# Order of VectorE's first work: two score tiles ahead of the second pair's residues, both value projections after the sixth tile

## Chip, cores and metric

The kernel runs on 1 core of a Trainium2 chip. The metric is the device time of one execution, in microseconds (us).

## What is computed

One transformer layer on x of 32 sequences x 256 tokens x 128 features, in float32: attention of 16 heads of 8 features with a causal mask and a distance penalty, then a gated feed-forward block of width 512, each followed by a residual sum and a layer norm. Cut to what matters here:

```python
Q = split_heads(x @ Wq.T + bq); K = split_heads(x @ Wk.T + bk); V = split_heads(x @ Wv.T + bv)
scores = jnp.einsum('bhid,bhjd->bhij', Q, K) / jnp.sqrt(jnp.float32(hd))
scores = jnp.where(causal_mask, -jnp.inf, scores) + decay
attn = jax.nn.softmax(scores, axis=-1)
out = jnp.einsum('bhij,bhjd->bhid', attn, V)
```

## The kernel before, in words

The 32 sequences are worked in 16 pairs; a pair is 512 tokens. Five engines take part, each in the order in which the program names its work: TensorE (PE), VectorE (DVE), ScalarE (ACT), GpSimd (POOL) and SyncE (SP, which issues most of the DMAs; ScalarE's queue issues the others). The wrapper `InOrder` (L50) keeps PE, DVE, ACT and SP in program order, and every instruction made through it carries the line L58 in the profile, so that one goes by the names of tiles.

**Queries and keys.** `project(n)` (L314) transposes a pair's x (`pxT`), copies it to SBUF on VectorE (`xT`), and multiplies it by the weights into `pq` and `pk`. `halves` (L295) splits each product into a leading part (`qhi`, `khi`, on ScalarE) and a residue (`qlo`, `klo`, on VectorE, which reads the product and the leading part). `stack` (L305) then spreads the four tiles by eight DMAs of 256 KB over interleaved rows of the big operands `qs` and `ks`: two for each of `qhi` and `qlo` on SP's queue, two for each of `khi` and `klo` on ScalarE's. Every score matmul contracts over all of these rows. Beforehand `fill` (L185) writes the constant rows.

**Row maxima.** A softmax needs each row's maximum first. `row_maxima(n, i)` (L373), with i from 0 to 11, computes one score tile (four matmuls of 62x128 by 62x256, or eight of 62x128 by 62x128 where i mod 3 is 2; then four small masking matmuls with `tri_q`) and reduces it on VectorE into `m`. `maxima_to_rows` (L407) transposes `m` (`pm`), splits it into `mhi` (ScalarE) and `mlo` (VectorE) and writes both into rows of `qs` by DMAs on SP. `weigh` (L430) then computes the scores again with the maxima in them, takes the exponential on ScalarE (`e`) and masks on GpSimd; `outputs` (L470) multiplies by the values.

**Values.** `project_values(n)` (L339) makes eight matmuls of 128x128 into `pv`; VectorE adds the bias in four instructions into `vaug`.

**Buffers.** Score tiles lie in three PSUM buffers (`ps_s`, L283) of 128x1024; `pxT`, `pq`, `pk`, `pv`, `pm` and the like share two buffers of 128x512 (`ps_w`, L284). So a fourth score tile waits for the first one's reduction, and a third `work` tile waits until the first has been read. The leading parts and residues of pair 1 lie in the pool `setup`, which is closed at L704; its memory is used again by `ep`, `op`, `yp` and `once`, the last of which takes the feed-forward weights.

**The start** (L684 to L720) is written out by hand. For VectorE, the order is: the operands of pair 0, `fill(qs[1])` (L694), the residues of pair 1 (within `run(ahead)`, L695), the values of pair 0 (L698), six tiles of maxima of pair 0 (L710), the values of pair 1 (L712), `maxima_to_rows(0, (0,))` (L713), `load_layers` (L714, the weights, on SP), six more tiles (L715), `maxima_to_rows(0, (1,))`, and two tiles of pair 1. After that `step(0)` begins, in which the pair's twelve `weigh` tiles alternate with pair 1's maxima, pair 2's projection (`project(2)`) and a count of weights that float32r can't hold (`differ`); then a branch, and steps 1 to 15.

Of the kernel before, what the change touches and what calls it, by code (L numbers as in the profile page):

```python
# [8 lines left out]
F32 = mybir.dt.float32  # L9
# [4 lines left out]
ALU = mybir.AluOpType  # L14
# [47 lines left out]
def tile_attn_ffn(  # L62
# [24 lines left out]
    pe, vec, act, sp = (InOrder(tc, e) for e in (nc.tensor, nc.vector, nc.scalar, nc.sync))  # L87
# [97 lines left out]
    def fill(dst, nm, eng, groups=slice(0, W)):  # L185
        t, base = fills[nm]
        to = dst[:, groups, :]
        t = t.unsqueeze(1).to_broadcast([P, groups.stop - groups.start, TOK])
        if eng is act:
            act.activation(to, t, AF.Identity, bias=base)  # L190
        else:
            eng.tensor_scalar(to, t, base, None, ALU.add)
# [93 lines left out]
    def work(nm):  # L286
        return ps_w.tile([P, 512], F32, name=nm, tag="work")

    def two(nm):
        return ps_s.tile([P, 2, 512], F32, name=nm, tag="s")  # L290
# [4 lines left out]
    def halves(n, ps, bias, nm):  # L295
        pool = setup if n == 1 else hlp
        hi = pool.tile([P, TOK], F32R, name=f"{nm}hi_{n}", tag=f"{nm}hi")
        act.activation(hi, ps, AF.Identity, bias=bias)
        lo = pool.tile([P, TOK], F32R, name=f"{nm}lo_{n}", tag=f"{nm}lo")
        vec.scalar_tensor_tensor(  # L300
            lo, ps, bias, hi.bitcast(F32), ALU.add, ALU.subtract
        )
        return hi, lo

    def stack(n, nm, eng=sp):  # L305
        for r, part in {
            "q": ((0, 0), (1, 0), (2, 1), (3, 1)), "k": ((0, 0), (2, 0), (1, 1), (3, 1))
        }[nm]:
            eng.dma_start(
                out=pairs[n][nm][PAIRING + r :: W, :, :].bitcast(F32),  # L310
                in_=pairs[n][nm + "s"][part].bitcast(F32),
            )

    def project(n):  # L314
        xn = xs[n]
        if n + 1 < NPAIR:
            xs[n + 1] = load_x(n + 1)
        pt = work(f"pxT_{n}")
        for t in range(NT):
            pe.transpose(pt[:, t * P : (t + 1) * P], xn[:, t, :], ident)  # L320
        xT = xtp.tile([P, TOK], F32, name=f"xT_{n}", tag="xT", bufs=2)
        vec.tensor_copy(xT, pt)

        for t in range(NT):
            nc.gpsimd.tensor_tensor(xn[:, t, :], xn[:, t, :], bo_sb, ALU.add)
        yield
        pq = work(f"pq_{n}")
        pe.matmul(pq, lhsT=wq_sb, rhs=xT, start=True, stop=True)
        q = halves(n, pq, bq_sb, "q")
        yield  # L330
        pk = work(f"pk_{n}")
        pe.matmul(pk, lhsT=wk_sb, rhs=xT, start=True, stop=True)
        k = halves(n, pk, bk_sb, "k")
        m = mp.tile([P, 2, 2, H], F32, name=f"m_{n}", tag="m")
        pairs[n] = dict(
            q=qs[n % 2], k=ks[n % 2], qs=q, ks=k, m=m, xT=xT, xb=xs.pop(n)
        )

    def project_values(n):  # L339
        xT, v = pairs[n]["xT"], vaug[n % 2]  # L340
        pairs[n]["v"] = v
        pv = work(f"pv_{n}")
        for t in range(NT):
            pe.matmul(
                pv[:, t * D : (t + 1) * D], lhsT=xT[:, t * P : (t + 1) * P], rhs=wv_sb,
                start=True, stop=True,
            )
        to = v[:, :, 0 : H // 2 * VSLOT].rearrange("p t (r c k) -> p t r c k", r=2, c=C)
        src = pv.rearrange("p (t r e c d) -> p t r e c d", t=NT, r=2, e=2, c=C)
        bias = bv_sb.rearrange("p (r e c d) -> p r e c d", r=2, e=2, c=C)  # L350
        for r in range(2):
            for e in range(2):
                vec.tensor_tensor(
                    to[:, :, r, :, 2 * e * VHEAD : 2 * e * VHEAD + HD], src[:, :, r, e],
                    bias[:, r, e].unsqueeze(1).to_broadcast([P, NT, C, HD]), ALU.add,
                )
# [3 lines left out]
    def mask(blocks):  # L360


        for p, f in ((0, 0), (1, 1), (0, 1), (1, 0)):
            s, first, count = blocks(p)
            rows = slice(64 * p, 64 * p + 64)
            pe.matmul(
                s[64 * f : 64 * f + 64, :, first + 64 * f : first + 64 * f + 64],
                lhsT=ident_b[rows, rows],
                rhs=tri_q[rows, rows].unsqueeze(1).to_broadcast([64, count, 64]),
                start=False, stop=True, tile_position=(64 * p, 64 * f),  # L370
            )

    def row_maxima(n, i):  # L373

        q, k, m = (pairs[n][w] for w in "qkm")
        mv = m.rearrange("i b c (e p g) -> i e p g b c", e=2, p=2)[:, i // 6]
        a, part = divmod(i, 3)
        if part < 2:
            g = 2 * a + part
            s = two(f"s1_{n}_{g}").rearrange("i p (b j) -> i p b j", b=2)  # L380
            for b in range(2):
                for p in range(2):
                    rows = slice(64 * p, 64 * p + ROWS1)
                    pe.matmul(
                        s[:, p, b, :], lhsT=q[rows, g, b * T + P : (b + 1) * T],
                        rhs=k[rows, g, b * T : (b + 1) * T], start=(b == 0), stop=False,
                    )
            mask(lambda p: (s[:, p], P, 2))
            vec.tensor_reduce(mv[:, :, g % C, :, 1], s, AX.X, ALU.max, negate=True)
            return  # L390
        s = two(f"s1_{n}_{a}d").rearrange("i p (h b j) -> i p h b j", h=2, b=2)
        for h in range(2):
            for b in range(2):
                for p in range(2):
                    rows = slice(64 * p, 64 * p + ROWS1)
                    i0 = b * T
                    pe.matmul(
                        s[:, p, h, b, :], lhsT=q[rows, 2 * a + h, i0 : i0 + P],
                        rhs=k[rows, 2 * a + h, i0 : i0 + P],
                        start=(h == 0 and b == 0), stop=False,  # L400
                    )
        mask(lambda p: (s[:, p].rearrange("i h b j -> i (h b) j"), 0, 4))
        vec.tensor_reduce(
            mv[:, :, 2 * a % C : 2 * a % C + 2, :, 0], s, AX.X, ALU.max, negate=True
        )

    def maxima_to_rows(n, halves=(0, 1)):  # L407

        q, m = pairs[n]["q"], pairs[n]["m"]
        pm = work(f"pm_{n}_{halves[0]}")  # L410
        e0, rows = halves[0], W * len(halves)
        for t in range(NT):
            pe.transpose(
                pm[0:rows, t * P : (t + 1) * P],
                m[:, t // 2, t % 2, W * e0 : W * e0 + rows], ident,
            )
        hi = mp.tile([H, TOK], F32R, name=f"mhi_{n}_{e0}", tag="mhi", bufs=1)
        act.copy(hi[0:rows, :], pm[0:rows, :])
        lo = mp.tile([H, TOK], F32R, name=f"mlo_{n}_{e0}", tag="mlo", bufs=1)
        vec.tensor_tensor(  # L420
            lo[0:rows, :], pm[0:rows, :], hi[0:rows, :].bitcast(F32), ALU.subtract
        )
        for i, e in enumerate(halves):
            for r, part in enumerate((hi, lo)):
                sp.dma_start(
                    out=q[ROWS1 + r :: 64, C * e : C * e + C, :].bitcast(F32),
                    in_=part[W * i : W * i + W, :].bitcast(F32),
                )
# [250 lines left out]
    def run(gen):  # L679
        for _ in gen:  # L680
            pass
# [11 lines left out]
    next(ahead)  # L693
    fill(qs[1], "q", vec)  # L694
    run(ahead)  # L695
    stack(1, "q", sp)
    stack(1, "k", act)
    project_values(0)  # L698
    for a in range(G):
        act.dma_start(  # L700
            out=wo_sb[C * HD * a : C * HD * (a + 1), :],
# [5 lines left out]
    yp = enter(tc.tile_pool(name="yp", bufs=2))  # L707
    lctx = ctx.enter_context(ExitStack())
    once = lctx.enter_context(tc.tile_pool(name="once", bufs=1))
    for i in range(6):  # L710
        row_maxima(0, i)
    project_values(1)  # L712
    maxima_to_rows(0, (0,))  # L713
    loaded = load_layers(once)  # L714
# [166 lines left out]
```

## Time and profile before

| | us |
|---|---|
| median of 3 runs (823.79 to 824.07) | 823.96 |
| the profiled execution's own time | 824.06 |
| its span, first to last instruction | 822.2 |
| PE busy in the span | 784.6 (95%) |
| DVE busy | 636.0 (77%) |
| ACT busy | 527.5 (64%) |
| PE busy from 11.0 to 20.7 us of the span | 5.55 of 9.70 |
| DVE busy in the same stretch | 5.07 of 9.70 |

A row of the timeline has the start in us from the span's start, the duration in us, the engine, the line, the operation, the tile written and those read with their shapes, and xN for N instructions merged; in brackets stands how long the engine had been idle before and what ended that. A row of the DMA view has a queue (q1 is fed by SP, q10 by ScalarE), packets, MB and the share of the 16 DMA engines' time. A row of the stage view has a stretch, its length, then for each engine the busy time in it, then the granted clock of TensorE (1.00 is full), the DMA share and GB/s.

### The profile page before, as it was taken

The numbers are of one execution on the slowest core, as the hardware profiler recorded it, in microseconds if no ns is written. First come the engines' busy times: TensorE is split into PE (matmuls) and PEld (weight loads), VectorE is DVE, ScalarE is ACT, GpSimd is POOL, SyncE is SP. The second block draws the span as 40 slices with busy tenths as digits, with TensorE's granted clock in tenths as the row PEclk, the third lists the DMA queues.
The fourth block names the chain that finished last, engine by engine and source line by source line (L and its number), as shares of the span: only waits on it lengthen the run. The fifth ranks groups of instructions, "written<-read, shape, count | busy, mean of one in ns | idle before, by whom it ended". The sixth has DMA issues, their size and how long they took to land.

```text
span 822.2 us, 17431 instructions
## 1 busy us (share of the span) xinstructions
PE 784.6 (95%) x7046; PEld 555.8 (68%) x7046; DVE 636.0 (77%) x1247; ACT 527.5 (64%) x719; POOL 260.8 (32%) x341
## 2 busy tenths in 40 slices
PE   4896999999999999999999999999999999999994
PEld 2664676776767677676767767676767767666673
DVE  6786778877887887778788877888878787873674
ACT  5065556766666766766576676667666666758572
POOL 5033413333142333414232342424243231424211
PEclk9879999999999999999999999999999999999998
DMA  6824140403204140410404040130404022000001
GB/s 147 213 62 106 29 92 14 106 15 74 60 14 106 28 107 14 92 42 21 110 17 106 27 101 20 43 90 15 107 26 104 4 62 59 14 4 14 1 8 37
DMA packets 39898, 47.49 MB, mean 58 GB/s; under 512 B 3968, under 2 KB 21632, under 8 KB 39808
## 3 DMA queue, kind: packets, MB, share of 16 engines
q1 hardware_dynamic: 37152, 42.82, 22.0%
q10 hardware_dynamic: 2656, 3.48, 1.9%
q8 instruction: 57, 0.93, 0.5%
q14 instruction: 33, 0.27, 0.1%
HBM read 7.48 MB, written 4.19 MB: 14 GB/s over the span
## 4 chain that ended last, share of the span: by engine, by line
PE 83%; DVE 4%; ACT 3%; issue 1%; DMA 0%; POOL 0%; ACTq 0%; POOLq 0%; DVEq 0%
PE peven L58 14%; PE podd L58 14%; PE s L58 12%; PE pa L58 11%; PE pw L58 10%; PE s_2d L58 2%; PE s_3d L58 2%; PE po L58 2%; PE s_0d L58 2%; PE s_1d L58 2%; PE pt L58 2%; PE pv L58 2%; PE pk L58 2%; PE pq L58 2%; PE px1T L58 1%; PE py L58 1%
## 5 line engine op out<-in xcount | busy, mean ns | idle before, releaser
L58 DVE TENSOR_REDUCE m<-s 128x4 f32<-128x1024 f32 x128 | 155.5, 1218 | 14.6 <-PE s L58 13.3
L58 ACT ACTIVATE e<-s 128x1024 f32<-128x1024 f32 x128 | 130.7, 1022 | 44.2 <-PE s L58 34.2
L463 POOL TENSOR_SCALAR_AFFINE_SELECT e<-e 128x512 f32<-128x512 f32 x128 | 82.6, 646 | 218.5 <-ACT e L58 189.3
L58 PE MATMUL podd<-h,h_near 128*128 128x512 f32 x512 | 131.3, 403 | 1.0 <-DVE m L58 0.5
L58 PE MATMUL peven<-hodd,h_near 128*128 128x512 f32 x512 | 122.7, 396 | 0.0
L58 PEld LDWEIGHTS peven<-hodd,h_near 128*128 128x128 f32 x512 | 95.7, 187 | 23.4 <-DVE hodd L58 0.3
L58 PEld LDWEIGHTS podd<-h,h_near 128*128 128x128 f32 x512 | 91.8, 188 | 23.1 <-DVE h L58 3.2
L58 ACT ACTIVATE hodd<-podd,sh 128x512 fp32r<-128x512 f32 x64 | 44.0, 688 | 62.7 <-PE podd L58 62.6
L58 PE MATMUL pw<-x1T,w_near 128*128 128x512 f32 x256 | 75.6, 418 | 1.1 <-DVE h0w L58 1.1
L274 POOL TENSOR_TENSOR rsa<-rsa,half 128x4 f32<-128x4 f32 x16 | 16.3, 1018 | 176.7 <-DVE rsa L58 176.7
L58 DVE SCALAR_TENSOR_TENSOR h0w<-pw,s,sg 128x512 f32<-128x512 f32 x64 | 47.9, 748 | 30.4 <-ACT sg L58 30.4
L58 PEld LDWEIGHTS s<-qs,ks 64*128 64x128 f32 x512 | 38.9, 188 | 47.7 <-issue 34.1
L58 PE MATMUL pa<-e,vaug 128*32 128x256 f32 x1024 | 70.6, 389 | 0.0
L58 PE MATMUL s<-qs,ks 64*128 64x256 f32 x512 | 65.3, 335 | 0.6 <-ACT e L58 0.5
L58 DVE TENSOR_TENSOR heven<-evenw,heven 128x512 fp32r<-128x512 f32 x64 | 44.2, 692 | 26.6 <-ACT evenw L58 26.1
L58 ACT ACT_TABLE_LOAD x47 | 60.3, 1283 | 3.4 <-issue 2.6
L58 ACT ACTIVATE sg<-pw,s 128x512 f32<-128x512 f32 x64 | 43.7, 684 | 28.2 <-PE pw L58 27.9
L58 PE MATMUL s<-ks,qs 62*128 62x256 f32 x512 | 56.9, 302 | 2.4 <-ACT e_0d L58 1.8
L58 ACT ACTIVATE heven<-peven,sh 128x512 fp32r<-128x512 f32 x48 | 33.4, 696 | 39.8 <-PE peven L58 39.8
L58 PEld LDWEIGHTS pw<-x1T,w_near 128*128 128x128 f32 x256 | 43.4, 188 | 18.4 <-ACT nothing L58 5.8
L581 POOL TENSOR_TENSOR h<-h0w,h 128x512 fp32r<-128x512 f32 x31 | 40.0, 1291 | 43.5 <-DVE h L58 41.2
L58 DVE TENSOR_TENSOR hodd<-oddw,hodd 128x512 fp32r<-128x512 f32 x64 | 43.7, 684 | 10.0 <-ACT oddw L58 9.9
(147 smaller groups left out, 1418.1 us busy)
## 6 DMA issues: line engine op xcount, KB each, us to landing
qs<-qhi SPq DMA_DIRECT2D x32, 256.0 KB
qs<-qlo SPq DMA_DIRECT2D x32, 256.0 KB
ks<-khi SPq DMA_DIRECT2D x26, 256.0 KB
ks<-klo SPq DMA_DIRECT2D x26, 256.0 KB
x<-in_x_dram SPq DMA_DIRECT2D x16, 256.0 KB
out_dram<-z SPq DMA_DIRECT2D x15, 256.0 KB
ks<-khi ACTq DMA_DIRECT2D x6, 256.0 KB
ks<-klo ACTq DMA_DIRECT2D x6, 256.0 KB
```

The source lines that it names most:

```text
L58: return lambda *args, **kw: self.tc.keep_in_program_order(call(*args, **kw))
L274: nc.gpsimd.tensor_tensor(rs, rs, half[:, 0:NT], ALU.pow)
L463: nc.gpsimd.affine_select(out=on_diagonal, in_=on_diagonal, pattern=[[0, on_diagonal.shape[1]], [1, P]], base=0, channel_multiplier=-1, co ...
L581: (nc.gpsimd if o < (1 if final else 2) else vec).tensor_tensor(h[:, 1, o, :], whole, h[:, 0, o, :].bitcast(F32), ALU.subtract)
```

## The change

`halves` no longer issues the residue at once but keeps it in a list `due`; for every pair but pair 1 the list is run on the spot, so nothing changes there. For pair 1 it is run after two tiles of maxima of pair 0. `project_values(0)` moves from in front of the six tiles to behind them, in front of `project_values(1)`.

```diff
@@ halves @@
         lo = pool.tile([P, TOK], F32R, name=f"{nm}lo_{n}", tag=f"{nm}lo")
-        vec.scalar_tensor_tensor(
-            lo, ps, bias, hi.bitcast(F32), ALU.add, ALU.subtract
-        )
+        due.append(
+            lambda: vec.scalar_tensor_tensor(lo, ps, bias, hi.bitcast(F32), ALU.add, ALU.subtract)
+        )
+        if n != 1:
+            run_due()
         return hi, lo
+    due = []
+
+    def run_due():
+        while due:
+            due.pop(0)()
@@ the start @@
     fill(qs[1], "q", vec)
     run(ahead)
+    for i in range(2):
+        row_maxima(0, i)
+    run_due()
     stack(1, "q", sp)
     stack(1, "k", act)
-    project_values(0)
...
-    for i in range(6):
+    for i in range(2, 6):
         row_maxima(0, i)
+    project_values(0)
     project_values(1)
     maxima_to_rows(0, (0,))
```

On VectorE the order from `fill(qs[1])` to `mlo` was: `qlo`, `klo`, four `vaug`, six reductions, four `vaug`, `mlo`. It is now: two reductions, `qlo`, `klo`, four reductions, eight `vaug`, `mlo`. On PE `pv` of pair 0 moves from in front of the first score tile to behind the sixth. The order on ScalarE, GpSimd and SP is the same, and so is the number of instructions on each engine.

## The prediction

> **What bounds the kernel now.** The page's first part gives PE 95% of the span, and its chain of work that ended last is 83% PE; but the change touches only the first 40 us, so I read that stage by itself: the PE and the DVE timeline from 0 to 45 us, then the DMA view up to the first score tile, then the stage view. PE before:
>
> ```profile
> 14.75 1.91 PE L58 MATMUL pk<-xT,wk_sb 128*128 128x512 f32 x2
> 20.02 2.08 PE L58 MATMUL pv<-wv_sb,xT 128*128 128x128 f32 x8 [3.36 <-DVE qlo L58]
> 22.03 0.79 PE L58 MATMUL s<-ks,qs 62*128 62x256 f32 x4
> 22.76 0.32 PE L58 MATMUL s<-tri_q,ident_b 64*64 64x128 bf16 x4
> ...
> 27.36 1.12 PE L58 MATMUL s_1d<-ks,qs 62*128 62x128 f32 x8
> 28.40 0.43 PE L58 MATMUL s_1d<-tri_q,ident_b 64*64 64x256 bf16 x4
> 28.76 2.07 PE L58 MATMUL pv<-wv_sb,xT 128*128 128x128 f32 x8
> 30.63 1.06 PE L58 MATMUL pm<-ident,m 128*8 128x128 f32 x4
> ```
>
> PE stands still from 16.66 to 20.02, and the first score tile runs only behind `pv`. VectorE:
>
> ```profile
> 19.22 0.75 DVE L58 SCALAR_TENSOR_TENSOR qlo<-pq,bq_sb,qhi 128x512 fp32r<-128x512 f32 x1 [4.01 <-ACT qhi L58]
> 19.89 0.74 DVE L58 SCALAR_TENSOR_TENSOR klo<-pk,bk_sb,khi 128x512 fp32r<-128x512 f32 x1
> 22.20 0.89 DVE L58 TENSOR_TENSOR vaug<-pv,bv_sb 128x128 f32<-128x128 f32 x4 [1.57 <-issue]
> 23.13 2.36 DVE L58 TENSOR_REDUCE m<-s 128x4 f32<-128x1024 f32 x2
> ...
> 28.92 1.22 DVE L58 TENSOR_REDUCE m<-s_1d 128x8 f32<-128x1024 f32 x1
> 30.94 0.89 DVE L58 TENSOR_TENSOR vaug<-pv,bv_sb 128x128 f32<-128x128 f32 x4 [0.81 <-PE pv L58]
> 32.33 0.68 DVE L58 TENSOR_TENSOR mlo<-pm,mhi 8x512 fp32r<-8x512 f32 x1 [0.51 <-ACT mhi L58]
> ```
>
> VectorE idles 4.01 us until 19.22: the gap that two reductions (2.36 us) could fill, if their score tiles were there. From 22.20 it is nearly without a break, and behind `mlo` six more reductions follow until 39.80 with no idle time, so here VectorE is the bound. Whether the gap can be used is decided by the operands: every score matmul reads all rows of `qs` and `ks`, so it needs all eight stacking DMAs of pair 0. DMA view, 11.0 to 20.7 us:
>
> ```profile
> q1 hardware_dynamic: 749, 1.14, 51.4%
> q10 hardware_dynamic: 576, 1.05, 47.5%
> ```
>
> Four DMAs of 256 KB are 1.05 MB per queue. q10 has moved its four (pair 0's keys) only by 20.7; of q1's 1.14 MB 0.09 is the x load queued behind its four. In the half microsecond from 20.5 q10 moved 4 packets more. **So the first score tile can't begin before about 20.7 us, 1.5 us after the gap has ended.** The cause of the gap is this transfer, and the change leaves it as it is.
>
> **The change, step by step.** No instruction is added or removed; ScalarE, GpSimd and SP keep their order. Each time below is a start plus durations of the rows above (successive starts give the pitch: 1.17 us per reduction, 0.67 per residue, 2.01 and 1.87 for `pv`, 1.05 and 1.40 for a score tile of either kind).
>
> 1. First tile: 20.7 + 1.05 = 21.75; reductions 21.8 to 24.15. Before, the first began at 23.13: 1.3 gained, since `vaug` (0.93) and `pv` no longer stand ahead.
> 2. `qlo`, `klo` now stand behind them: 24.15 to 25.5. Before, these 1.35 us lay inside the wait for the transfer and cost nothing; now they lie in the row of work. Four more reductions: 25.5 to 30.1, against 30.14 before. Nothing is left of the gain.
> 3. PE: the sixth tile needs the buffer of the third, whose reduction now ends at 26.7 (behind the residues), so it runs 26.7 to 28.1, not 27.36 to 28.76. Then both `pv`: 28.1 to 32.0. Before, one of them (2.0) lay in the wait until 22.03.
> 4. VectorE: first four `vaug` 30.15 to 31.05, a pause for the second `pv`, the others 32.05 to 32.95. `pm` begins at 32.0 (it needs the first `pv`'s buffer, free at 31.05, and PE, which is the later), against 30.63. Its cost is 1.06 at the slow rate (its own row) or 0.66 at the fast one (the four transposes `pt` at 61.92); the fast rate sets in at about 32.3, as in the `s` rows before (0.79 at 31.62, 0.50 at 32.52), so I take 0.75. Then `mhi` (0.57) and `mlo` at 33.4, against 32.33: **1.07 us later**. With `pm` slow throughout it would be 1.4, with `pm` fast throughout 1.0.
> 5. What is late next: the six reductions behind `mlo` have no idle time before them, so they end 1.07 later, and `pm` of the second half begins at 40.9, not 39.86. SP's weight loads behind `mlo` move along.
>
> Of the waits moved: the DMAs of `klo` on ScalarE's queue now wait until 25.5; behind them stand four for `wo` and then `mhi`. Their rows before are 2.50 and 4.11 us, so 25.5 + 0.2 + 2.50 + 4.11 = 32.3, against `mhi` wanted at 32.75: hidden, with 0.4 to spare. If the issues took 1 us longer, `mhi` would be 0.6 late. `qlo`'s DMAs on SP block nothing until `qs<-mhi` at 33.3. Pair 1's stack then lands near 32 instead of 31; its first reader runs at 40.8 before, so 8 us cover it, and the weight loads that reuse its memory come at 34.7.
>
> **TensorE's clock.** Behind 39.9 us PE is the bound, and at half clock:
>
> ```profile
> 39.90:52.80 12.90, 12.90 (x101) 8.54 (x101) 10.83 (x15) 6.68 (x9) 5.11 (x8) 0.50 0.41 130
> 52.80:66.80 14.00, 13.16 (x185) 8.11 (x182) 12.20 (x24) 11.88 (x17) 5.04 (x7) 1.00 0.01 2
> ```
>
> PE is busy for 12.90 of 12.90 us at 0.50, and then the clock rises. In the 0.1 us rows of the stage view it falls at 35.7, rises at 52.8 and falls at 73.3: 17.1 and 20.5 us apart, 5 and 6 steps of 3.41. So it changes on a grid, and not whenever PE is busy. What lifted it: the last step before 52.8 held `pa` (1.9 us, 128 rows); that before 49.4 held 1.1 us of `pxT` among score tiles of 62 rows and lifted nothing. Moved by 1.07, the step that ends at 52.8 keeps only 0.8 us of `pa`. If the grid stands where it stood, the clock then rises at 56.2. The price: `pa` ends at 52.77 + 1.07 = 53.84, `pq` takes 1.9 (its pitch at half clock, 12.88 to 14.75) instead of 1.1, so pair 2's `qlo`, for which VectorE idled 1.77 until 54.65, begins 1.07 + 0.85 = 1.9 later. From 54.65 VectorE has work to 68.3 with pauses of 0.1 us at most, so that is passed on; the chain of waits then goes from VectorE's last reduction of pair 1 (65.56) through `pm` and `mhi` to the branch.
>
> The Trainium skill (TensorE: Matmul & The Clock Gate, "What's actually happening") states that one busy window of about 3.4 us lifts the throttle and that the window is free-running. The stretch above, busy throughout at 0.50 for 12.9 us, speaks against the first; by that rule the clock would follow the work and the sum would be 1.07, or 825.1; by the row it is 1.9, and the measurement decides. The second, if it holds, puts the grid elsewhere in each execution; no row of a single trace shows it.
>
> **Sum.** 1.07 + 0.85 = 1.9 us later. The profiled execution has 824.06, 1.86 more than its span and 0.10 above the median; 824.06 + 1.9 = 826.0, or **825.9** against the median.
>
> **Rivals.** What a measurement of this kernel can tell from no change is about 0.2%, 1.65 us.
>
> - *A, forecast: the order costs 1.07 and the clock rises one step later.* +1.65 to +2.8, about 825.9.
> - *B: the order costs 1.07 and the clock gives some back.* If it still rises at 52.8, the last 1.07 us of `pa` shrink to 0.6 and `pq` to 1.1: `qlo` 0.65 later. Or it stays full at 73.3, where the grid step before would hold 1.7 us of `pa` instead of less: `pv` there took 1.7 us at half clock where 1.0 would do, 0.7 back from A's 1.9. +0.4 to +1.6, about 825.1. For it: PE's margin is one step, and the margin is thin. Against: a shift of 1 us moves most of `pa` out of the step.
> - *C, faster: the score tiles start in the gap after all.* Each us by which the first tile begins before 20.7 moves step 1 to 5 forward by as much; even at 19.6, and faster by 1.65 from 18.0 on; at best 2.36, the two reductions within the gap (821.6). Against it: by the same view in steps, q10 had moved 0.85 of its 1.05 MB by 19.0.
> - *D: ScalarE's issues or a second step of half clock come on top.* `mhi` late by 0.6 to 1.5, or another 3.4 us at half clock, at 0.4 lost per us (0.66 against 1.06 for four transposes): +3 to +5, about 828.
>
> **Chances.** A 0.48, B 0.40, C 0.06, D 0.06. B is within 0.2%, so slower 0.54, same 0.40, faster 0.06. The range 824.3 to 827.0 holds A and B and leaves out C and D.
>
> **What the changed profile would show.** PE's idle time before the first `s` is about 4.0, ended by a stacking DMA, with the start at 20.7; the first reduction at 21.8 with 6.6 idle before it; `qlo` at 24.2; both `pv` side by side from 28.1; `mlo` at 33.4; `pm` of the second half at 40.9; the granted clock at 0.50 until 56.2 (A) or 52.8 (B); pair 2's `qlo` at 56.6 (A) or 55.3 (B). I am wrong if the first `s` starts before 19.6, if PE at half clock isn't the bound between 40 and 54, or if the whole delay is taken up by a wait between 68 and 78 that doesn't move with the work.

## The result

The changed kernel took 825.4 us (median of 20 runs, 824.7 to 826.42) against 823.91 us before (20 runs, 822.83 to 824.98): the ratio is 1.0018, 95% interval 1.0012 to 1.0024. So it is 1.5 us slower: the interval leaves out no change, but the size is just inside the 0.2% that the prediction took as the bound of "same". The profiled execution took 825.69 us with a span of 823.7 us.

PE in the profile after, the rows that answer to those of before:

```profile
21.76 0.80 PE L58 MATMUL s<-ks,qs 62*128 62x256 f32 x4 [5.73 <-DMA ks<-klo]
...
27.72 1.12 PE L58 MATMUL s_1d<-ks,qs 62*128 62x128 f32 x8 [0.56 <-DVE m L58]
...
29.13 3.78 PE L58 MATMUL pv<-wv_sb,xT 128*128 128x128 f32 x16
32.70 0.79 PE L58 MATMUL pm<-ident,m 128*8 128x128 f32 x4
...
41.65 1.01 PE L58 MATMUL pm<-ident,m 128*8 128x128 f32 x4 [2.50 <-DVE m L58]
...
54.56 2.08 PE L58 MATMUL pq<-xT,wq_sb 128*128 128x512 f32 x2
```

The first score tile now waits 5.73 us, and the releaser is named: a stacking DMA. It starts at 21.76, only 0.27 earlier than before (22.03). Both `pv` (x16) stand between the sixth tile and `pm`. VectorE:

```profile
22.86 2.36 DVE L58 TENSOR_REDUCE m<-s 128x4 f32<-128x1024 f32 x2 [8.09 <-PE s L58]
25.13 0.74 DVE L58 SCALAR_TENSOR_TENSOR qlo<-pq,bq_sb,qhi 128x512 fp32r<-128x512 f32 x1
...
31.29 0.89 DVE L58 TENSOR_TENSOR vaug<-pv,bv_sb 128x128 f32<-128x128 f32 x4 [0.24 <-issue]
33.01 0.88 DVE L58 TENSOR_TENSOR vaug<-pv,bv_sb 128x128 f32<-128x128 f32 x4 [0.83 <-PE pv L58]
34.13 0.68 DVE L58 TENSOR_TENSOR mlo<-pm,mhi 8x512 fp32r<-8x512 f32 x1 [0.23 <-ACT mhi L58]
...
57.40 0.75 DVE L58 SCALAR_TENSOR_TENSOR qlo<-pq,bq_sb,qhi 128x512 fp32r<-128x512 f32 x1 [2.72 <-ACT qhi L58]
```

VectorE's pause has not been filled: it has grown from 4.01 to 8.09 us, and `qlo` now follows it. `mlo` is at 34.13 instead of 32.33: **1.80 us later**. The second half's `pm` is at 41.65 instead of 39.86 (1.79 later): passed on whole. Pair 2's `qlo` is 2.75 later (57.40 against 54.65). The last 0.95 of that is the clock: `pq`, from which `qlo` is made, took 2.08 us and not 1.12. Before:

```profile
52.77 1.12 PE L58 MATMUL pq<-xT,wq_sb 128*128 128x512 f32 x2
...
54.65 0.75 DVE L58 SCALAR_TENSOR_TENSOR qlo<-pq,bq_sb,qhi 128x512 fp32r<-128x512 f32 x1 [1.77 <-ACT qhi L58]
```

The stage view after, in steps of 0.1 us, has the rise here:

```profile
56.90:57.00 0.10, 0.10 (x4) 0.10 (x4) 0.00 (x0) 0.10 (x1) 0.00 (x0) 0.68 0.00 0
57.00:57.10 0.10, 0.10 (x6) 0.10 (x6) 0.00 (x0) 0.10 (x1) 0.00 (x0) 1.00 0.00 0
```

The clock (third column from the right) is full from 57.0, against 52.8 before. Further on some is given back: the last transposes (`py`) start at 814.37 instead of 812.01, 2.36 later, and the span is 1.5 longer.

### The profile page after: what moved, and what is told of

It reads as the page before. It is cut to its first block, busy times and chain, and to the rows that moved or that the text cites. A ratio compares the mean times of both kernels' runs of the same rounds, so it can differ in the third digit from the quotient of the medians.

```text
span 823.7 us, 17431 instructions
## 1 busy us (share of the span) xinstructions
PE 782.6 (95%) x7046; PEld 553.5 (67%) x7046; DVE 636.0 (77%) x1247; ACT 527.1 (64%) x719; POOL 260.4 (32%) x341
## 4 chain that ended last, share of the span: by engine, by line
PE 82%; DVE 4%; ACT 3%; issue 1%; DMA 1%; POOL 0%; SPq 0%; ACTq 0%; POOLq 0%; DVEq 0%
PE peven L58 14%; PE podd L58 14%; PE s L58 12%; PE pa L58 11%; PE pw L58 10%; PE s_2d L58 2%; PE s_3d L58 2%; PE s_0d L58 2%; PE s_1d L58 2%; PE po L58 2%; PE pt L58 2%; PE pk L58 2%; PE pq L58 2%; PE pv L58 2%; PE px1T L58 1%; PE py L58 1%
```

## The experiments

Theory: the two tiles cannot use VectorE's pause because their operands land at 21.8 us; behind them the residues, and behind six tiles one of the two value projections, lose the wait that hid them. Rivals: one half of the change alone carries the cost; the order is bad whatever the tiles wait for; only the clock differs. The medians, each beside the kernel before on the same chip:

| run | median us | before | ratio, interval | first `mlo` |
|---|---|---|---|---|
| e1_residues_only | 827.93 | 823.75 | 1.0049, 1.0033 to 1.0065 | 36.31 |
| e2_values_only | 825.19 | 823.75 | 1.0012, 1.0 to 1.0024 | 33.61 |
| e3_half_stack_new | 821.11 | 823.75 | 0.9966, 0.995 to 0.9982 | 30.06 |
| e4_half_stack_old | 819.37 | 823.75 | 0.9953, 0.9929 to 0.9976 | 27.84 |
| e7_free_tiles_new | 822.56 | 823.52 | 0.9982, 0.9968 to 0.9996 | 31.72 |
| e8_free_tiles_old | 823.88 | 823.52 | 1.0001, 0.9992 to 1.0011 | 32.14 |
| e5_values_in_pause | 822.78 | 823.52 | 0.999, 0.9979 to 1.0001 | 32.27 |
| e9_values_in_wait | 821.03 | 824.07 | 0.996, 0.9945 to 0.9975 | 31.76 |
| e10_klo_on_sp | 823.85 | 824.07 | 0.9991, 0.9976 to 1.0007 | 32.14 |

**The two halves of the change.** e1, from the changed kernel:

```diff
     stack(1, "k", act)
+    project_values(0)
...
     for i in range(2, 6):
         row_maxima(0, i)
-    project_values(0)
     project_values(1)
```

> Only half of the change: two score tiles ahead of the second pair's residues, but the first pair's value projection back in front of tiles 3 to 6. Theory (the first tile waits for the stacking DMAs until 21.8 us, so the residues and the value projection lose the wait that hid them): pv now needs the buffer that qlo frees at 25.8 and stands on PE ahead of the third tile, so that tile runs at 27.9, the sixth at 31.3, and mlo comes at 36.3 instead of 32.3: about +4.0 us, 827.9 (827.2 to 828.7 with the clock grid). Rival 1 (the moved values are the cost, the residues are harmless): as before, 823.9. Rival 2 (only the clock grid differs): within 0.7 us of before.

Measured: 827.93, and `mlo` at 36.31, both as the theory had them. PE of e1:

```profile
25.96 2.08 PE L58 MATMUL pv<-wv_sb,xT 128*128 128x128 f32 x8 [2.14 <-DVE qlo L58]
27.97 1.11 PE L58 MATMUL s_0d<-ks,qs 62*128 62x128 f32 x8
```

`pv` waits for the buffer that `qlo` frees, and the third tile stands behind it. So moving `pv` along was needed: the residues alone would have cost more than twice as much as the whole change. e2, from the kernel before:

```diff
     stack(1, "k", act)
-    project_values(0)
...
     for i in range(6):
         row_maxima(0, i)
+    project_values(0)
     project_values(1)
```

> The other half: residues where they were, both value projections behind the sixth tile. Theory: residues hidden again (19.2 to 20.6), first tile still at 21.8, reductions 22.9 to 29.8, both pv from 28.5, mlo at 33.2 to 33.9 instead of 32.3: about +1.2 us, 825.1; the rest of the change's cost, 0.3 to 0.9 us, is the residues. Rival 1 (the moved values are the whole cost): as the changed kernel or slower, 825.4 or more. Rival 2 (only the clock grid differs): within 0.7 us of before. A rival on the residues alone: as before.

Measured: 825.19. PE of e2:

```profile
21.62 0.79 PE L58 MATMUL s<-ks,qs 62*128 62x256 f32 x4 [5.60 <-DMA ks<-klo]
...
28.35 3.78 PE L58 MATMUL pv<-wv_sb,xT 128*128 128x128 f32 x16
```

Here the residues are in the pause and `mlo` comes at 33.61. Of the 1.80 us, 33.61 - 32.33 = 1.28 are thus the moved projection, and 34.13 - 33.61 = 0.52 the residues. The split holds with the projection moved first: from e1's side the residues alone cost 3.98, and moving the projection too takes 2.18 of that back. The projection's cost arises on PE: the tiles can begin 0.41 earlier than at 22.03, but 1.9 us of `pv` have left the wait. The medians (1.4 of about 1.5) can't part the two: e2's interval begins at no change, and by them alone rival 1, the moved values as the whole cost, would stand. The split rests on `mlo`.

**An earlier landing, first try.** e3 and e4 leave out half of pair 0's stacking:

```diff
         }[nm]:
+            if n == 0 and part == 1:
+                continue
             eng.dma_start(
```

> The changed kernel, leaving out the four stacking DMAs of the first pair's residue halves (those rows of its queries and keys stay at the constants that were filled in), so that 1 MB instead of 2 MB must land before the first score tile. Theory: the operands are there at about 17.4 us, the two reductions fall into VectorE's gap (18.5 to 20.9), and mlo comes at about 30.1: 2.2 us (1.5 to 2.9) faster than the old order with the same four DMAs left out. Rival (the new order is worse whatever lands when): slower than it by 1.5 us.

> The kernel before, leaving out the same four stacking DMAs. Theory: there the first score tile stands behind pv and not on the transfer, which ends at 22.0, so the earlier landing is worth nothing: 823.9 within 0.7 us, mlo still at 32.3. Rival (the transfer bounds the old order as well): the first tile and mlo come 3 to 4 us earlier, about 820.5.

The new order gained what was expected (`mlo` at 30.06, first tile at 17.42), but the old one gained 4.4 us where nothing was expected, and stayed the faster by 1.7. Read by itself, that is the rival's number, and e4's total, too, is nearer to its rival's 820.5 than to 823.9. The ScalarE timeline shows why the pair is no clean test. Before, and then e4:

```profile
12.00 2.86 ACTq L58 DMA_DIRECT2D ks<-klo  x2
14.90 3.71 ACT L58 ACTIVATE ks<-kconst,col_k_base 128x4096 fp32r<-128x4096 f32 x1 [4.35 <-issue]
```

```profile
11.96 3.71 ACT L58 ACTIVATE ks<-kconst,col_k_base 128x4096 fp32r<-128x4096 f32 x1 [1.38 <-issue]
15.57 0.67 ACT L58 ACTIVATE qhi<-pq,bq_sb 128x512 fp32r<-128x512 f32 x1
```

The two `klo` DMAs that were left out hold ScalarE for 2.86 us while they are issued. Without them the fill, `qhi` and with it `qlo` come 2.9 us earlier (16.27), and VectorE's pause, which was to be filled, is gone: 1.06 us are left of it. The experiment had moved both ends.

**An earlier landing, clean.** e7 and e8 leave every DMA and every other instruction in place and let only the two tiles read other operands:

```diff
+                    lq, rk = q[rows, g, :], k[rows, g, :]
+                    if n == 0 and i < 2:
+                        lq, rk = (pairs[0][w][0][rows, :] for w in ("qs", "ks"))
                     pe.matmul(
-                        s[:, p, b, :], lhsT=q[rows, g, b * T + P : (b + 1) * T],
-                        rhs=k[rows, g, b * T : (b + 1) * T], start=(b == 0), stop=False,
+                        s[:, p, b, :], lhsT=lq[:, b * T + P : (b + 1) * T],
+                        rhs=rk[:, b * T : (b + 1) * T], start=(b == 0), stop=False,
                     )
```

> The changed kernel, with the first two score tiles computed from the leading halves qhi and khi of the first pair instead of the stacked operands (so their maxima are not those of the scores), with the same shapes: these two tiles then wait for no stacking DMA, and every DMA and every other instruction stays where it is. Theory (the order loses because its tiles wait for the transfer): the tiles run behind pk at about 16.2 us, their two reductions fall into VectorE's gap and end at about 20, the third tile starts at 21.8 with the landing, and mlo comes at about 31.9 instead of 34.1: total -0.4 us against the kernel before (-1.2 to +0.4), about 823.4. Rival (the order of the residues and values is bad whatever the tiles wait for): still 1 us or more slower than before, 824.8 to 825.4.

> The kernel before with the same two tiles computed from qhi and khi. Theory (there the tiles stand behind pv until 22.0, when the operands have landed anyway): no change, 823.8 within 0.6 us, mlo at 32.3. Rival (the old order waits for the transfer as well): faster by up to 1 us.

e7, with the new order, was faster than the kernel before (822.56 against 823.52); e8, with the old one, was the same, and 1.3 us behind e7. (The profiled execution of e7 took 827.63 us, its other twelve 821.13 to 823.39; that of e8 took 826.83, its other eleven 822.4 to 825.11. Only their first 40 us are read here.) VectorE in e7, then PE in e8, where the freed tile still stands behind `pv`:

```profile
15.10 2.36 DVE L58 TENSOR_REDUCE m<-s 128x4 f32<-128x1024 f32 x2 [0.28 <-PE s L58]
19.23 0.75 DVE L58 SCALAR_TENSOR_TENSOR qlo<-pq,bq_sb,qhi 128x512 fp32r<-128x512 f32 x1 [1.77 <-ACT qhi L58]
...
31.72 0.68 DVE L58 TENSOR_TENSOR mlo<-pm,mhi 8x512 fp32r<-8x512 f32 x1 [0.40 <-ACT mhi L58]
```

```profile
21.84 0.79 PE L58 MATMUL s<-khi,qhi 62*128 62x256 f32 x4
```

In e7 both reductions lie in the pause, `qlo` is back at 19.23, and `mlo` comes 2.41 us earlier than in the changed kernel. So the wait for the operands, and not the order as such, makes the change lose; the rival falls.

**The clock.** The kernel before was profiled a second time.

> The kernel before, unchanged, profiled once more to see where TensorE's clock changes. If the grid of the clock's changes moves freely from one execution to the next, the rises and falls stand at other places than 32.3, 35.7, 52.8 and 73.3 us (still 3.41 us or multiples apart), while the instructions up to 40 us start within 0.3 us of where they did. Rival (the grid is tied to the kernel's start): the same places.

It took 824.72 us. Its stage view and its VectorE:

```profile
55.20:55.30 0.10, 0.10 (x4) 0.10 (x4) 0.00 (x0) 0.10 (x1) 0.00 (x0) 0.54 0.00 0
55.30:55.40 0.10, 0.10 (x6) 0.10 (x4) 0.00 (x0) 0.10 (x1) 0.00 (x0) 1.00 0.00 0
```

```profile
55.55 0.75 DVE L58 SCALAR_TENSOR_TENSOR qlo<-pq,bq_sb,qhi 128x512 fp32r<-128x512 f32 x1 [2.72 <-ACT qhi L58]
```

With the same program, and the second `pm` at 39.81 as before (39.86), the clock rises at 55.3 and not at 52.8, and pair 2's `qlo` is 0.90 later. Its clock falls at 34.8 and 82.6 us, 6 and 8 steps of 3.41 from the rise, so the grid has the same step at another place. The other traces bear this out. Counted from the start of the first `pa`, the rise came after 1.9 us in the first profile of the kernel before, 4.4 in e6, 4.3 after the change, 3.0 in e10 and 4.8 in e8; over all twelve profiles it was 1.7 to 5.6. So the grid moves from one execution to the next, the first profile had an early rise, and one more step of half clock is no property of the change. Against e6 the changed kernel's `qlo` is 57.40 - 55.55 = 1.85 later, about the order's 1.80; in these two executions the rise happened to lie 1.7 apart, so that the clock adds next to nothing.

**Using the wait.** If the landing can't be had earlier, work that needs no stacked operand should lie in the wait. e5 moves pair 1's projection to PE's pause in front of the second `pm`:

```diff
-    for i in range(6):
+    for i in range(8):
         row_maxima(0, i)
-    project_values(1)
     maxima_to_rows(0, (0,))
     loaded = load_layers(once)
-    for i in range(6, 3 * G):
+    for i in range(8, 3 * G):
         row_maxima(0, i)
+    project_values(1)
     maxima_to_rows(0, (1,))
```

> The kernel before, with two more tiles of maxima ahead of the first half's transposed maxima, and the second pair's value projection moved into PE's pause of 1.9 us between the twelfth tile and the second half's pm (VectorE's part into its pause of 1.7 us before the second mlo). Theory (in the stretch from 21.7 to 40 us an engine loses only where it waits, and pv and vaug of the second pair cost VectorE 1.3 us of pauses in front of the first mlo): the second mlo comes at 40.1 instead of 41.5, total -1.3 us (-0.5 to -2.1), about 822.5. Rival (PE at half clock is the bound throughout, so a moved pv costs the same elsewhere): no change, 823.8.

The second `mlo` came at 39.90 instead of 41.52, 1.6 earlier, which speaks against the rival as far as this `mlo`; but the total (0.7 less) cannot be told from no change by its interval. e10 moves only the two `klo` DMAs that hold ScalarE; e9 does that too, puts both projections into the wait and keeps e5's eight tiles:

```diff
-            eng.dma_start(
+            (sp if n == 0 and part else eng).dma_start(
...
     project_values(0)
+    project_values(1)
...
-    for i in range(6):
+    for i in range(8):
         row_maxima(0, i)
-    project_values(1)
     maxima_to_rows(0, (0,))
     loaded = load_layers(once)
-    for i in range(6, 3 * G):
+    for i in range(8, 3 * G):
```

> The kernel before with only the first pair's two klo DMAs moved to SP's queue. Theory: qlo comes at 16.3 and pv runs within the wait, but the first score tile is still held by the landing at 21.8 (22.0 before), so only 0.3 us is gained: 823.3 (822.5 to 823.8). Rival (the old order was bounded by qlo and pv, not by the landing): 2 to 3 us gained, about 821.

> Uses the wait for the transfer for work that doesn't need the stacked operands. From the kernel before: the first pair's two klo DMAs go to SP's queue, so that ScalarE's fill and qhi, khi of the second pair no longer stand behind their issue; both value projections stand ahead of all score tiles; eight tiles instead of six ahead of the first half's pm. Theory: qlo at 16.3, both pv from 17 to 21, both vaug done by 21.9, first tile still at 21.8 with the landing, then PE runs through; the second mlo comes at 37.3 to 38.5 instead of 41.5: total -2.4 us (-1.4 to -3.2), about 821.2. Rival (the moved DMAs make the landing later by as much as is gained): no change, 823.6.

e10 was as before within its interval. PE in e10:

```profile
17.12 1.16 PE L58 MATMUL pv<-wv_sb,xT 128*128 128x128 f32 x8 [1.09 <-DVE qlo L58]
21.84 0.80 PE L58 MATMUL s<-ks,qs 62*128 62x256 f32 x4 [3.56 <-DMA ks<-klo]
```

`pv` came at 17.12, but the first tile still at 21.84, held by the landing. That the old order was bounded by `qlo` and `pv` alone is thereby refuted: the two bounds lie 0.2 to 0.4 us apart (22.03 before, 21.84 here, 21.62 in e2). e9 took 821.03 against 824.07, **3.0 us faster than the kernel before** and the fastest of those that leave nothing out. PE in e9:

```profile
17.19 2.30 PE L58 MATMUL pv<-wv_sb,xT 128*128 128x128 f32 x16 [0.42 <-DVE qlo L58]
21.96 0.50 PE L58 MATMUL s<-ks,qs 62*128 62x256 f32 x4 [2.47 <-DMA ks<-klo]
```

Both projections have run before the landing, in the 5 us for which PE had waited, and the second `mlo` came at 38.67 instead of 41.52. How the 3.0 us divide over e9's three edits was not tested: e10 shows only that the moved DMAs alone gain nothing that can be told. A small part is TensorE's clock: the first tile's matmuls ran in 0.50 us here (0.80 in e10), and the first reduction began 0.74 us behind the tile's start (1.09 in e10).

## Why the prediction was right, and where it was not

The forecast was slower, +1.9 us (825.9); measured were +1.5, within its range, but under its own bound of 0.2%, so that "same" would have been the better call. By size it lies in rival B's band (+0.4 to +1.6) and not in A's (+1.65 to +2.8). The mechanism of the order held, at 0.73 us more than its sum; the 0.85 us for the clock were no cost of the change. That the two errors nearly cancel is luck.

- **The cause of the pause is the transfer.** Right: the first tile's releaser is a stacking DMA, and e7 shows the sign turn when that wait is taken away.
- **Step 1, the first tile at 20.7.** Mis-sized: it was 21.76. The bytes were as read. DMA view after, 11.0 to 20.7 us, and then 20.7 to 21.7 us, whose only queue is q1 (a share adds up the packets' times, so it can pass 100%):

```profile
q10 hardware_dynamic: 576, 1.05, 47.7%
```

```profile
q1 hardware_dynamic: 423, 0.27, 119.0%
```

  q10's four are through by 20.7 and nothing of it moves in the next microsecond, yet PE starts 1.06 us after that. The end of the packets was taken for the time at which a reader may start; e1, e2, e7 and e10 (21.79, 21.62, 21.77, 21.84) repeat it, with 1.0 to 1.15 us from the last packet of `klo` to PE. In the trace's record of semaphores the last update by `klo`'s DMAs comes at 21.46, 0.8 us behind the packet and 0.3 ahead of PE. The Trainium skill (DMA: Bandwidth & Descriptors, "Anatomy of one DMA — SWDGE (gpsimd) path") puts most of a DMA's fixed cost of about 2 us into the confirmation that the last byte has landed; it says so of another issuing path than SP's and ScalarE's, but the 1.06 us here agree with it in kind. What fills them no run here shows.
- **Steps 2 to 4, the sum 1.07.** The residues' and the projection's parts were right in kind: e1 and e2 came within 0.3 us of sums made by the same steps once 21.76 was put in (+4.2 where +4.0 was expected, +1.4 where +1.2 was). The start added 1.06; the two `pv` took 3.57 instead of 3.9, 0.3 less. Together 1.80 instead of 1.07.
- **Step 5**, passed on whole: right (1.79 at the second `pm`).
- **The clock, +0.85.** The price was right (0.90 between two profiles of the kernel before, 0.95 here), but it was no consequence of the change, as e6 shows. The step that failed is "if the grid stands where it stood": a single trace was taken for the rule. What lifts the clock stays open, too: the prediction looked to the time of 128-row matmuls in a step, but in e3 a step with 2.2 us of them (`pa` from 48.62 on, then `pq`) lifted nothing, while in e4 one with 1.7 us of `pa` did. The 825.1 that it names for the page's rule counts from the profiled execution; from the median it is 825.0. The two rules of the Trainium skill weighed there (TensorE: Matmul & The Clock Gate, "What's actually happening") part ways: that the window is free-running agrees with e6; that one busy window lifts the throttle does not, since after the change, too, PE was busy from 41.65 to 57.0 without a break at half clock.
- **ScalarE's issues, rival D.** Not so: 2.7 us to spare instead of 0.4, as the last section tells.

Open stays how the 1.80 us at 34 us become 1.5 in the median. In the profiled pair the delay was 2.36 at `py` (1.97 against e6, where `py` starts at 812.40), and the issue of the last two output DMAs took 1.34 us instead of 2.24, which makes the span's 1.5; whether the medians go the same way was not measured.

## What to carry to other kernels

An idle stretch is free only for work whose operands are there: before work is moved into a pause, find what ends last among its inputs, DMA landings too, and count a landing from the end of its wait and not from its last packet. Work that sits in somebody else's wait costs nothing there, though it looks as if it stood in the way; when it is moved out, its price appears (here 1.28 us for a projection of about 2). The reverse, moving independent work into the wait, was one of the three edits of e9, which together gained 3.0 us.

## What the runs showed of the hardware that was not expected

- The issue of a DMA can hold the engine that issues it, and for how long varies: pair 1's two `klo` DMAs and the four `wo` DMAs took 2.50 and 4.11 us of ScalarE before, and 1.55 and 2.68 after, when they came some 5 us later; in e10 they took 1.55 and 6.07. What sets the length was not tested. After:

```profile
26.56 1.55 ACTq L58 DMA_DIRECT2D ks<-klo  x2
28.15 2.68 ACTq L58 DMA_DIRECT2D wo_sb<-in_woT_dram  x4
33.52 0.57 ACT L58 CAST mhi<-pm 8x512 fp32r<-8x512 f32 x1 [13.94 <-PE pm L58]
```

- The places at which TensorE's clock changes move between executions of the same program, at a cost of 0.9 us at pair 2's `qlo` here, which is of the size of the change under study. Medians of many runs were needed for a difference of 1.5 us.
